# Second front's Abs and Exp spread over scan steps, q and k weights scaled in other buffers, and the last net with the last pair's outputs computed by halves of the tokens

## The chip, the cores and the metric

The kernel runs on one core of one Trainium2 chip. The metric is the device time of one execution in microseconds (us); lower is better. All data are 32-bit floats. The engines are named as the profile names them: PE (TensorE, matmuls; PEld is its weight loading), DVE (VectorE), ACT (ScalarE), POOL (GpSimd), SP (SyncE, which only issues DMAs here).

## The reference

Eight sequences of 512 tokens with 256 features go through two layers, each with a layer norm ahead of and behind it and a residual. The first is a state-space layer, the second a mixture-of-experts attention with a feed-forward net.

```python
# layer 1, per sequence: D_INNER = 512 channels, 16 states each
dt = softplus(dt_r @ dt_proj_w.T + dt_proj_b)
h  = exp(dt * A) * h + dt * B * xc          # scan over 512 tokens
y  = (h @ C + xc * D) * silu(z) @ out_proj_w.T
x  = x + norm(y)
# layer 2, per sequence: H = 16 heads of 64, E = 8 experts, top 2 by gate
q, k = rope(src @ Wq), rope(src @ Wk);  gv, go = gate(src)
o    = softmax(q @ k.T / 8) @ (sum over e of gv[e] * (src @ Wv[e]))
src  = ln1(src + sum over heads, e of go[e] * o @ Wo[e])
src  = ln2(src + relu(src @ W1 + b1) @ W2 + b2)     # W1: 256 x 1024
out  = x + norm(src)
```

## The kernel before

**Order.** PE, DVE, ACT and POOL execute in the order in which the program issues to them. That order is made while the program is built: `_Order` (line 98) keeps a clock `now` of planned PE time, and every piece of work is a generator or a callback with a due time. `pe(us)` books PE time, each DVE call books its own cost (`_Vector`, line 165), `yield us` asks to go on so much later, `Free` marks pieces that may go on without waiting for free DVE time. What is due is issued at that point, so a different due time is a different place in the queue of an engine. DMAs are issued by SP (most) and POOL (the accumulating ones); SP's order is left to the framework's scheduler, and its queue is in order as well: an issue that waits for a buffer holds all later ones.

**Buffers.** A pool hands out its buffers per tag in turn: `wpool` two of each tag (`wqk`, `w_m`, `wv`, `wo`, `gb`), `work` two of each (`p`, `ve`, `og`), `big` seven, `half` five, `one` a single one per tag (`dt`, `dtx`, `xc`, `pt`, `o`, `qk`). `psum` has three tiles of two banks, `psum_a` one, which holds the sum over all heads (`sums[b]`).

**State-space layer.** For sequence b, `front(b)` (line 315) makes the inputs and `mamba(b)` (line 492) scans. The scan has 32 steps; a step takes one of 4 blocks of 128 channels and 2 of 16 states, tile 128x1024. A step is one DVE scan (`h<-da,ps_u` or `h<-da,h`) and one DVE product with `ct`, and for later sequences a product ahead of it; ACT makes the decays `da` (two Exp) of the next step; POOL issues two DMAs that add the products into `xc` (line 566). Scan 0 runs nearly alone. During it `front(1)` prepares sequence 1: its Abs (line 457) and Exp (line 459), two groups of two Abs and one Exp, go to ACT between the decays.

**Weights of q and k.** `later_constants` (line 266) loads the q and k weights of each of 8 head pairs into a tile of tag `wqk`, scales the q part on ACT (line 289) and stores it to DRAM `wqk_d` (line 290); from the third on it waits until sequence 0 is in `state`. `Pair.project` (line 803) loads the scaled weights back, into a tile of the same tag.

**Attention.** 8 pairs of heads per sequence. `ahead` (line 1101) issues a pair's values `ps_v`, scores `ps_s`, transposes `ps_pt` and the next pair's projection `ps_qk`, and between them the eight outputs of the pair before, `add_output(k)` (line 967): for each expert two matmuls of 512 tokens into `sums[b]`. Their inputs `og` are DVE products of the pair's result `o` with the gates `gb`, which SP broadcasts from DRAM (`weigh`, line 954).

**Net.** `feed_forward(b)` (line 992) runs among the pairs of sequence b + 1: residual sum, transposes to tokens, norm, transposes to features, `ps_f` with W1 (line 1040) and with W2 (line 1062) in two halves of F, norm, norm, output. For the last sequence nothing is left beside it: after the last pair come its eight outputs and then the net, one after the other.

Of the kernel before, what the change touches and what calls it, by code (L numbers as in the profile page):

```python
# [26 lines left out]
F32 = mybir.dt.float32  # L27
AF = mybir.ActivationFunctionType
ALU = mybir.AluOpType
# [3 lines left out]
P = 128  # L33
B, S, D = 8, 512, 256
ND = D // P
NT = S // P
# [3 lines left out]
H, HP, E, F = 16, 64, 8, 1024  # L40
NF = F // P
# [15 lines left out]
NET, FIRST = -9, 0.2  # L57
# [40 lines left out]
class _Order:  # L98
# [11 lines left out]
    def pe(self, us):  # L110
        self.now += us
        self.here = self.now
# [4 lines left out]
    def after(self, us, do):  # L117

        heapq.heappush(self.queue, (self.here + us, self.n, do))
        self.n += 1  # L120
# [95 lines left out]
def _layers(  # L216
# [3 lines left out]
    nc = tc.nc  # L220
    with ExitStack() as ctx:
        pool = lambda name, bufs, **kw: ctx.enter_context(tc.tile_pool(name=name, bufs=bufs, **kw))
        const = pool("const1", 1)
        wpool = pool("weights", 2)
        seq = pool("seq", 2)
        big = pool("big", 7)
        half = pool("half", 5)
        work = pool("work", 2)
        one = pool("one", 1)
# [7 lines left out]
        x1_d = [tc.dram_tile([P, NT, D], F32, name=f"x1_d_{b}") for b in range(B)]  # L237
# [13 lines left out]
        b1_t = const.tile([P, NF], F32, name="b1_t")  # L251
        rows_t = const.tile([P, 4, D], F32, name="rows_t")
# [13 lines left out]
        def later_constants():  # L266

            nc.sync.dma_start(out=w_sel, in_=wsel)
            nc.sync.dma_start(out=angle[:, :, 0, :], in_=rope)
            half_turn = half.tile([P, P], F32, tag="half", name="half_turn")  # L270
            nc.sync.dma_start(out=half_turn, in_=turn)
            nc.sync.dma_start(out=b1_t, in_=b1)
            nc.sync.dma_start(
                out=rows_t.rearrange("p r d -> p (r d)"),
                in_=rows[:, : 4 * D].to_broadcast([P, 4 * D]),
            )
            yield 8.0


            vector.tensor_reduce(sign, half_turn, AX.X, ALU.add)  # L280
            vector.tensor_scalar(angle[:, 1, 0, :], angle[:, 1, 0, :], sign, None, ALU.mult)

            for i in range(H // 2):
                w = wpool.tile([P, 2, ND, P], F32, tag="wqk", name=f"wqk_s_{i}")
                nc.sync.dma_start(out=w, in_=wqk[i])
                yield 6.0
                while i > 1 and 0 not in state:
                    yield Free(2.0)
                nc.scalar.mul(w[:, 0], w[:, 0], HP**-0.5)
                nc.sync.dma_start(out=wqk_d[i], in_=w)  # L290

        def banks(name):
            return psum.tile([P, 2, S], F32, tag="mm", name=name)
# [18 lines left out]
        state = {}  # L312
        pe, after, then = order_of.pe, order_of.after, order_of.then

        def front(b):
# [4 lines left out]
            free = Free if b == 1 else float  # L320
# [16 lines left out]
            ps = to_features(xn, f"m_{b}")  # L337
# [40 lines left out]
            for m in range(0, NC, 2):  # L378
                ps = project(m)
# [4 lines left out]
            if b == 0:  # L384
                ps = project(NC)
# [42 lines left out]
            if b == 0:  # L428
                ps = project(NC + 2)
# [4 lines left out]
            if b == 0:  # L434
# [8 lines left out]
            nc.sync.dma_start(  # L443
                out=row, in_=bc_d[b][2 * NS : 2 * NS + 1, :].to_broadcast([P, S])
            )
            yield free(1.0)
            if b > 1:
                yield from gate()
            yield free(2.0)
# [4 lines left out]
            for m in range(0, NC, 2):  # L454
                u = tile_for(f"u_{b}_{m}", "og")
                for i in range(2):
                    nc.scalar.activation(u[:, i, :], row, AF.Abs, **step_size(m + i))
                yield free(1.4)
                nc.scalar.activation(u, u, AF.Exp, scale=-1.0)
                us.append(u)  # L460
                yield free(1.1)
            while b == 1 and at["step"] < steps - 1:
                yield Free(0.5)
            for u in us:
                m = 2 * len(lns)
                spare = b == 0 and m
# [10 lines left out]
            for ln, u in zip(lns, us):  # L477
                m = 2 * lns.index(ln)
                for i in range(2):
                    w = half.tile([P, S], F32, tag="half", name=f"w_{b}_{m + i}")  # L480
# [308 lines left out]
        class Pair:  # L789
# [3 lines left out]
            def __init__(self, b, pair):  # L793
                self.b, self.pair, self.id = b, pair, f"{b}_{pair}"
                self.xt = inputs_of[b]
                self.p, self.og = {}, {}

                self.done = set()

            def need(self, *what):  # L800
# [129 lines left out]
            def attend(self):  # L930


                self.need(*((of, t) for of in ("pt", "v") for t in range(NT)))
                po = banks(f"ps_o_{self.id}")
                for t in range(NT):
                    for j in range(2):
                        nc.tensor.matmul(  # L937
                            po[j * HP : j * HP + HP, 0, :], lhsT=self.v[:, j, t, :],
                            rhs=self.pt[:, j, t, :], start=(t == 0), stop=(t == NT - 1),
                        )  # L940
                pe(4.4)
                self.o = one.tile([P, 1, S], F32, tag="o", name=f"o_{self.id}")
                nc.scalar.copy(self.o, po[:, 0:1, :])  # L943
                for q in range(2):
                    after(0.8 + 0.1 * q, lambda q=q: self.weigh_soon(q))

            def weigh_soon(self, q):
# [5 lines left out]

            def weigh(self, q):

                gb = wpool.tile([P, 2, S], F32, tag="gb", name=f"gb_{self.id}_{q}")
                for j in range(2):
                    r = (2 * self.pair + j) * E + 2 * q
                    nc.sync.dma_start(
                        out=gb[j * HP : j * HP + HP].rearrange("p e s -> p (e s)"),  # L960
                        in_=go_d[self.b][r : r + 2, :].rearrange("e s -> (e s)")
                        .unsqueeze(0).to_broadcast([HP, 2 * S]),
                    )
                og = self.og[q] = work.tile([P, 2, S], F32, tag="og", name=f"og_{self.id}_{q}")
                vector.tensor_tensor(og, self.o.to_broadcast([P, 2, S]), gb, ALU.mult)

            def add_output(self, k):

                if self.pair == 0 and k == 0:
                    sums[self.b] = psum_a.tile([P, ND, S], F32, tag="sum", name=f"ps_a_{self.b}")  # L970
                pa, q, i = sums[self.b], k // 2, k % 2
                order_of.run(lambda: q in self.og)
                if i == 0:
                    w = self.wo = wpool.tile(
                        [P, 2, D], F32, tag="wo", name=f"wo_{self.id}_{q}"
                    )
                    for j in range(2):
                        nc.sync.dma_start(
                            out=w[j * HP : j * HP + HP],
                            in_=wo[2 * self.pair + j][:, q, :].rearrange("(i p) d -> p i d", i=2),  # L980
                        )
                for c in range(ND):
                    nc.tensor.matmul(  # L983
                        pa[:, c, :], lhsT=self.wo[:, i, bass.ts(c, P)], rhs=self.og[q][:, i, :],
                        start=(self.pair == 0 and k == 0),
                        stop=(self.pair == H // 2 - 1 and k == E - 1),
                    )
                pe(1.71)
                if i == 1 and q + 2 < E // 2:
                    after(0.05, lambda: self.weigh(q + 2))  # L990

        def feed_forward(b, pa):

# [90 lines left out]
            nc.sync.dma_start(out=out[b].rearrange("(t p) d -> p t d", p=P), in_=z)  # L1084
            finished.add(b)

        sums, prepared, inputs_of = {}, {}, {}  # L1090
        scanning, scanned, through, gated, summed, finished = (set() for _ in range(6))
# [22 lines left out]
                    part()  # L1114
                order_of.run()

        last = None
        with tc.manual_schedule(engines=MANUAL):
            first = front(0)
            order_of.start(first, 0, next(first))  # L1120
            order_of.start(mamba(0), 0)
            order_of.start(front(1), FIRST, 9.0)
            first_constants()
            order_of.run(lambda: 0 in scanning)
            order_of.start(later_constants(), NET)
            order_of.run(lambda: 0 in inputs_of)
            pairs = {}
            follow(-1, H // 2 - 1)
            for b in range(B):
                for pair in range(H // 2):  # L1130
                    now = pairs.pop((b, pair))
                    ahead(now, lambda: follow(b, pair))
                    if pair == 0 and b:
                        order_of.start(feed_forward(b - 1, sums[b - 1]), NET)
                    now.attend()
                    order_of.run()
                    last = now
            for k in range(E):
                last.add_output(k)
                order_of.run()  # L1140
            order_of.start(feed_forward(B - 1, sums[B - 1]), NET)
            order_of.run(lambda: not (order_of.queue or order_of.rest))


# [81 lines left out]
```

## Time and profile before

| | us |
|---|---|
| median of 3 runs | 3695.3 |
| lowest, highest | 3694.61, 3702.96 |
| the profiled execution, its own time | 3698.07 |
| its span, first to last instruction | 3696.3 |
| busy PE, DVE, POOL, ACT | 3413.1, 3047.2, 1681.2, 1645.2 |

The profile shows one execution. A wait is named by the instruction that waits and what it waited for; the chain that ended last follows the end of the span back from each instruction to what released it. A matmul of 32-bit data is two instructions of the profile, so `add_output` shows as four rows of 128x512. The page cuts the span in 40 slices of 92.4 us: PE is busy below 90% in the first five (state-space layer of sequence 0, first pairs) and in the last, which holds the last outputs and the last net.

### The profile page before, as it was taken

Reading aid. Unit: us, or ns where it says so; the run is one execution under the profiler, and the core shown is the slowest. Engines: PE = TensorE matmul, PEld = TensorE weight load, DVE = VectorE, ACT = ScalarE, POOL = GpSimd, SP = SyncE. Lnnn points to the kernel's source line nnn. Section 1 sums busy time; section 2 is a strip of 40 time slices with the busy share of each in tenths; the row PEclk is TensorE's granted clock in tenths of the full one; section 3 lists DMA queues with packets and bytes.
Section 4 is the critical chain, followed back from the end, with each engine's and each line's share of the span. In section 5 each row is a group of like instructions: output and inputs, shape, how many; then the busy total and the mean of one; then the engine's idle time right before and its main releaser. Section 6 shows DMA issues by size and latency. Waiting matters only on the chain.

```text
span 3696.3 us, 34548 instructions
## 1 busy us (share of the span) xinstructions
PE 3413.1 (92%) x10956; PEld 1626.4 (44%) x10956; DVE 3047.2 (82%) x3190; ACT 1645.2 (45%) x2798; POOL 1681.2 (45%) x1593
## 2 busy tenths in 40 slices
PE   5768889999999999999999999999999999999996
PEld 3633334444344444444444544434444444445443
DVE  7878998799989898999989998899988998754443
ACT  5524443545543455344544446443653444332331
POOL 1415663354645545454454545355444556232230
PEclk7879999999999999999999999999999999999998
DMA  4937774576866768477755868568765777344431
GB/s 144 196 93 183 174 176 119 149 186 166 195 150 162 179 168 196 121 182 177 199 142 142 201 149 209 138 152 194 183 168 132 179 191 175 99 120 112 111 92 57
DMA packets 285604, 578.48 MB, mean 157 GB/s; under 512 B 37608, under 2 KB 124904, under 8 KB 285424
## 3 DMA queue, kind: packets, MB, share of 16 engines
q1 hardware_dynamic: 204656, 427.33, 40.0%
q0 software_dynamic: 80768, 148.95, 24.1%
q8 instruction: 89, 1.46, 0.2%
q14 instruction: 91, 0.75, 0.1%
HBM read 405.72 MB, written 21.51 MB: 116 GB/s over the span
## 4 chain that ended last, share of the span: by engine, by line
PE 47%; DVE 26%; issue 8%; DMA 7%; ACT 5%; POOL 5%; SPq 0%; DVEq 0%; POOLq 0%; ACTq 0%
PE ps_v L907 14%; PE ps_a L983 12%; DVE h L175 11%; PE ps_qk L810 5%; DMA xc<-h 5%; PE ps_s L848 4%; PE ps_o L937 3%; PE ps_pt L883 3%; DVE ve L175 2%; DVE og L175 2%; DVE low L175 2%; PE ps_f L1040 1%; DVE xs L175 1%; DVE hit L175 1%; POOL ve L923 1%
## 5 line engine op out<-in xcount | busy, mean ns | idle before, releaser
L983 PE MATMUL ps_a<-og,wo 128*128 128x512 f32 x2048 | 967.1, 605 | 32.8 <-DVE og L175 32.5
L907 PE MATMUL ps_v<-wv,xt 128*128 128x512 f32 x2048 | 946.8, 606 | 21.4 <-DVE y L175 13.2
L923 POOL TENSOR_TENSOR ve<-ve 128x512 f32<-128x512 f32 x256 | 425.3, 1661 | 1144.9 <-DVE ve L175 994.7
L863 ACT ACTIVATE p<-ps_s,low 128x512 f32<-128x512 f32 x512 | 347.3, 683 | 723.6 <-DVE low L175 723.1
L566 POOL DMA_DIRECT2D xc<-h x504 | 465.1, 1103 | 384.7 <-DMA xc<-h 174.6
L907 PEld LDWEIGHTS ps_v<-wv,xt 128*128 128x128 f32 x2048 | 385.6, 193 | 544.8 <-issue 484.2
L983 PEld LDWEIGHTS ps_a<-og,wo 128*128 128x128 f32 x2048 | 373.1, 192 | 506.4 <-issue 429.0
L175 DVE TENSOR_TENSOR_SCAN h<-da,h 128x1024 f32<-128x1024 f32 x228 | 541.0, 2373 | 10.2 <-ACT da L503 0.2
L872 ACT ACTIVATE p<-p,total 128x512 f32<-128x512 f32 x512 | 341.5, 714 | 260.8 <-DVE total L175 260.4
L175 DVE TENSOR_TENSOR og<-o,gb 128x1024 f32<-128x1024 f32 x256 | 319.7, 1269 | 130.3 <-ACT o L943 72.4
L175 DVE TENSOR_TENSOR ve<-ps_v,gv 128x1024 f32<-128x1024 f32 x256 | 311.4, 1216 | 126.5 <-PE ps_v L907 99.3
L889 ACT COPY pt<-ps_pt 128x1024 f32<-128x1024 f32 x256 | 256.9, 1005 | 356.5 <-PE ps_pt L883 355.2
L503 ACT ACTIVATE da<-dt,decay 128x511 f32<-128x511 f32 x512 | 339.7, 713 | 104.6 <-DVE h L175 101.8
L175 DVE TENSOR_TENSOR h<-bt,dtx 128x1024 f32<-128x1024 f32 x228 | 321.2, 1409 | 33.7 <-DMA xc<-h 28.6
L175 DVE TENSOR_TENSOR h<-h,ct 128x1024 f32<-128x1024 f32 x256 | 339.1, 1324 | 3.8
L175 DVE TENSOR_REDUCE low<-ps_s 128x2 f32<-128x1024 f32 x256 | 310.4, 1213 | 26.6 <-PE ps_s L848 25.6
L924 POOL TENSOR_TENSOR ve<-ve 128x256 f32<-128x256 f32 x256 | 319.2, 1247 | 20.1
L832 POOL DMA_DIRECT2D qk<-sin x256 | 204.7, 1212 | 264.5 <-DVE qk L175 127.2
L848 PE MATMUL ps_s<-qk 64*128 64x512 f32 x1024 | 294.2, 650 | 23.7 <-ACT p L863 12.8
L883 PEld LDWEIGHTS ps_pt<-ident,p 128*128 128x128 f32 x2048 | 239.5, 141 | 132.0 <-issue 94.8
L937 PE MATMUL ps_o<-pt,v 128*64 128x512 f32 x1024 | 248.3, 611 | 29.0 <-POOL v L925 16.4
L883 PE MATMUL ps_pt<-ident,p 128*128 128x128 f32 x2048 | 266.7, 273 | 7.6 <-ACT p L872 3.3
(134 smaller groups left out, 3340.3 us busy)
## 6 DMA issues: line engine op xcount, KB each, us to landing
gb<-go_d SPq DMA_DIRECT2D x512, 256.0 KB, 4.9
xc<-h POOLq DMA_DIRECT2D x504, 256.0 KB, 5.7
wv<-in_wv_dram SPq DMA_DIRECT2D x128, 512.0 KB, 5.7
wo<-in_wo_dram SPq DMA_DIRECT2D x512, 128.0 KB, 4.0
ct<-bc_d SPq DMA_DIRECT2D x64, 512.0 KB, 5.9
bt<-bc_d SPq DMA_DIRECT2D x57, 512.0 KB, 5.2
wqk<-wqk_d SPq DMA_DIRECT2D x64, 256.0 KB, 2.6
qk<-sin POOLq DMA_DIRECT2D x256, 64.0 KB, 4.7
```

The source lines that it names most:

```text
L175: return getattr(self.engine, name)(*args, **kw)
L503: nc.scalar.activation(das[k % 2][:, j, 1:S], dt[:, m, 1:S], AF.Exp, scale=decay[:, m, g + j : g + j + 1],)
L566: nc.gpsimd.dma_start(out=xc[:, k % NC, :], in_=hs[k][:, j, :], accum_op=ALU.add)
L848: nc.tensor.matmul(ps[:, j, :], lhsT=self.qk[feats, 0, bass.ts(t, P)], rhs=self.qk[feats, 1, :], start=True, stop=True,)
L863: nc.scalar.activation(p[:, j, :], ps[:, j, :], AF.Exp, bias=low[:, j : j + 1], accum_out=total[:, j : j + 1],)
L872: nc.scalar.mul(p[:, j, :], p[:, j, :], total[:, j : j + 1])
L883: nc.tensor.transpose(pp[:, j, bass.ts(i, P)], self.p[t][:, j, bass.ts(i, P)], ident)
L907: nc.tensor.matmul(ps[:, i, :], lhsT=self.xt[:, c, bass.ts(t + i, P)], rhs=self.wv[:, c, :], start=(c == 0), stop=(c == ND - 1),)
L923: nc.gpsimd.tensor_tensor(ve[:, :, 0:4], ve[:, :, 0:4], ve[:, :, 4:8], ALU.add)
L924: nc.gpsimd.tensor_tensor(ve[:, :, 0:2], ve[:, :, 0:2], ve[:, :, 2:4], ALU.add)
L937: nc.tensor.matmul(po[j * HP : j * HP + HP, 0, :], lhsT=self.v[:, j, t, :], rhs=self.pt[:, j, t, :], start=(t == 0), stop=(t == NT - 1),)
L983: nc.tensor.matmul(pa[:, c, :], lhsT=self.wo[:, i, bass.ts(c, P)], rhs=self.og[q][:, i, :], start=(self.pair == 0 and k == 0), stop=(self. ...
```

## The change

Three edits. (1) `front(1)` waits longer in planned time ahead of its Abs and Exp and between them. (2) The tiles for scaling q and k weights take tag `w_m` in place of `wqk`, and from the third on the wait is for the gates of sequence 0 and stands ahead of the load. (3) For the last sequence, outputs are added by halves of the 512 tokens (`add_half`: matmuls of 256 tokens), the residual enters the sum as a matmul with the identity, and a function `last_net` replaces the last outputs and `feed_forward(7)`: it issues its loads at the start of the last sequence's second pair, into the buffers of `dt`, `dtx` and `xc`, and then runs outputs, norms, W1 and W2 for one half of the tokens beside the other.

```diff
@@ later_constants @@
             for i in range(H // 2):
-                w = wpool.tile([P, 2, ND, P], F32, tag="wqk", name=f"wqk_s_{i}")
+                while i > 1 and 0 not in gated:
+                    yield Free(2.0)
+                w = wpool.tile([P, 2, ND, P], F32, tag="w_m", name=f"wqk_s_{i}")
                 nc.sync.dma_start(out=w, in_=wqk[i])
                 yield 6.0
-                while i > 1 and 0 not in state:
-                    yield Free(2.0)
                 nc.scalar.mul(w[:, 0], w[:, 0], HP**-0.5)
                 nc.sync.dma_start(out=wqk_d[i], in_=w)
@@ front @@
-            yield free(1.0)
+            yield free(12.0 if b == 1 else 1.0)
...
                     nc.scalar.activation(u[:, i, :], row, AF.Abs, **step_size(m + i))
-                yield free(1.4)
+                yield free(3.5 if b == 1 else 1.4)
                 nc.scalar.activation(u, u, AF.Exp, scale=-1.0)
                 us.append(u)
-                yield free(1.1)
+                yield free(3.5 if b == 1 else 1.1)
@@ Pair @@
+                self.final = b == B - 1 and pair == H // 2 - 1
...
-                for q in range(2):
+                for q in range(E // 2 if self.final else 2):
                     after(0.8 + 0.1 * q, lambda q=q: self.weigh_soon(q))
...
-                gb = wpool.tile([P, 2, S], F32, tag="gb", name=f"gb_{self.id}_{q}")
+                spare = self.final and q > 1
+                of, tag = (work, "ve") if spare else (wpool, "gb")
+                gb = of.tile([P, 2, S], F32, tag=tag, name=f"gb_{self.id}_{q}")
...
-                og = self.og[q] = work.tile([P, 2, S], F32, tag="og", name=f"og_{self.id}_{q}")
+                og = self.og[q] = work.tile(
+                    [P, 2, S], F32, tag="p" if spare else "og", name=f"og_{self.id}_{q}"
+                )
...
+                if self.b == B - 1:
+                    for g in range(2):
+                        self.add_half(k, g, self.wo[:, i])
+                else:
...
+            def add_half(self, k, g, w):
+                pa = sums[self.b].rearrange("p g (c s) -> p g c s", c=ND)[:, g]
+                if self.pair == 0 and k == 0:
+                    nc.tensor.matmul(
+                        pa, lhsT=ident, rhs=self.xt[:, :, bass.ts(g, S // 2)],
+                        start=True, stop=False,
+                    )
+                    pe(0.86)
+                for c in range(ND):
+                    nc.tensor.matmul(
+                        pa[:, c, :], lhsT=w[:, bass.ts(c, P)],
+                        rhs=self.og[k // 2][:, k % 2, bass.ts(g, S // 2)],
+                        start=False, stop=(self.final and k == E - 1 and c == ND - 1),
+                    )
@@ new @@
+        def last_net():
+            b = B - 1
+            w_1 = one.tile([P, ND, F], F32, tag="dt", name="w1_last")
+            w_2 = one.tile([P, NF, D], F32, tag="dtx", name="w2_last")
+            w_o = one.tile([P, E // 2, 2, D], F32, tag="xc", name="wo_last")
+            x1 = big.tile([P, NT, D], F32, tag="big", name="x1_last")
+            b2 = half.tile([P, 1, D], F32, tag="half", name="b2_last")
+            for j in range(2):
+                nc.sync.dma_start(
+                    out=w_o[j * HP : j * HP + HP],
+                    in_=wo[H - 2 + j].rearrange("(i p) q d -> p q i d", i=2),
+                )
+            nc.sync.dma_start(out=w_1, in_=w1)
+            nc.sync.dma_start(out=w_2, in_=w2)
+            nc.sync.dma_start(out=x1, in_=x1_d[b])
+            nc.sync.dma_start(out=b2[:, 0, :], in_=rows[:, 4 * D :].to_broadcast([P, D]))
+            yield
+            pa = sums[b].rearrange("p g (c s) -> p g c s", c=ND)
+            half_of = lambda name: [
+                big.tile([P, ND, S // 2], F32, tag="big", name=f"{name}_last_{g}") for g in (0, 1)
+            ]
+            wide = [P, NT // 2, D]
+            rows_of = lambda i: rows_t[:, i : i + 1, :].to_broadcast(wide)
+            acc, y, yt = half_of("acc"), half_of("y"), half_of("yt")
+            hid = one.tile([P, NF, S], F32, tag="pt", name="hid_last")
+            def outputs(g, ks):
+                for k in ks:
+                    order_of.run(lambda: k // 2 in last.og)
+                    last.add_half(k, g, w_o[:, k // 2, k % 2])
+                    pe(0.86)
+                    order_of.run()
+            def to_tokens(g):
+                ps = banks("ps_acc_last")[:, 0, :].rearrange("p (t d) -> p t d", d=D)
+                for t in range(NT // 2):
+                    for c in range(ND):
+                        nc.tensor.transpose(
+                            ps[:, t, bass.ts(c, P)], acc[g][:, c, bass.ts(t, P)], ident
+                        )
+                nc.scalar.copy(y[g], ps)
+            def normed(g, *then):
+                for _ in norm(y[g], [y[g][:, t, :] for t in range(NT // 2)]):
+                    pass
+                for a, op in then:
+                    vector.tensor_tensor(y[g], y[g], a, op)
+            def features(g):
+                ps = banks("ps_tr_f_last")
+                for c in range(ND):
+                    for t in range(NT // 2):
+                        nc.tensor.transpose(
+                            ps[:, c, bass.ts(t, P)], y[g][:, t, bass.ts(c, P)], ident
+                        )
+                nc.scalar.copy(yt[g], ps[:, :, : S // 2])
+                vector.tensor_tensor(y[g], y[g], b2.to_broadcast(wide), ALU.add)
+            def hidden(g, f):
+                ps = banks("ps_f1_last").rearrange("p a (i s) -> p (a i) s", s=S // 2)
+                for i in range(4):
+                    for c in range(ND):
+                        nc.tensor.matmul(
+                            ps[:, i, :], lhsT=w_1[:, c, bass.ts(f + i, P)], rhs=yt[g][:, c, :],
+                            start=(c == 0), stop=(c == ND - 1),
+                        )
+                for i in range(4):
+                    nc.scalar.activation(
+                        hid[:, f + i, bass.ts(g, S // 2)], ps[:, i, :], AF.Relu,
+                        bias=b1_t[:, f + i : f + i + 1],
+                    )
+            def second(g):
+                ps = banks("ps_f2_last")[:, 0, :].rearrange("p (t d) -> p t d", d=D)
+                for t in range(NT // 2):
+                    for f in range(NF):
+                        nc.tensor.matmul(
+                            ps[:, t, :], lhsT=hid[:, f, bass.ts(g * NT // 2 + t, P)],
+                            rhs=w_2[:, f, :], start=(f == 0), stop=(f == NF - 1),
+                        )
+                vector.tensor_tensor(y[g], y[g], ps, ALU.add)
+                normed(g, (rows_of(2), ALU.mult), (rows_of(3), ALU.add))
+                tiles = slice(g * NT // 2, (g + 1) * NT // 2)
+                normed(g, (x1[:, tiles, :], ALU.add))
+                nc.sync.dma_start(
+                    out=out[b].rearrange("(t p) d -> p t d", p=P)[:, tiles, :], in_=y[g]
+                )
+            first = ((rows_of(0), ALU.mult), (rows_of(1), ALU.add))
+            outputs(0, range(E))
+            outputs(1, range(2))
+            nc.scalar.copy(acc[0], pa[:, 0])
+            outputs(1, range(2, 4))
+            to_tokens(0)
+            outputs(1, range(4, E))
+            normed(0, *first)
+            nc.scalar.copy(acc[1], pa[:, 1])
+            features(0)
+            to_tokens(1)
+            hidden(0, 0)
+            normed(1, *first)
+            hidden(0, 4)
+            features(1)
+            for f in range(0, NF, 4):
+                hidden(1, f)
+            for g in range(2):
+                second(g)
@@ main loop @@
-        last = None
+        last, net = None, last_net()
...
                 for pair in range(H // 2):
+                    if (b, pair) == (B - 1, 1):
+                        next(net)
...
-            for k in range(E):
-                last.add_output(k)
-                order_of.run()
-            order_of.start(feed_forward(B - 1, sums[B - 1]), NET)
-            order_of.run(lambda: not (order_of.queue or order_of.rest))
+            order_of.run(lambda: not order_of.rest)
+            next(net, None)
```

## The prediction

> **What bounds the kernel now.** I read the page's busy line and its 40 slices first, then PE's waits, then the timelines of the three places that the edits touch.
>
> ```profile
> PE 3413.1 (92%) x10956; PEld 1626.4 (44%) x10956; DVE 3047.2 (82%) x3190; ACT 1645.2 (45%) x2798; POOL 1681.2 (45%) x1593
> ...
> PE   5768889999999999999999999999999999999996
> ```
>
> PE bounds all but the ends: slices 6 to 39 are at 90% or more. Three places can give time without less matmul work: scan 0 (the 5 and 7, bound by DVE), the few waits of the early pairs, and the last slice.
>
> Scan 0 is bound by DVE: a step takes 3.45 us there, and PE waits for it. In DVE's and ACT's timelines the second front's Abs and Exp show as a stall of one step:
>
> ```profile
> 123.10 2.29 DVE L175 TENSOR_TENSOR_SCAN h<-da,ps_u 128x1024 f32<-128x1024 f32 x1 [3.13 <-ACT da L503]
> ```
> ```profile
> 117.83 1.52 ACT L457 ACTIVATE u<-row,chan,w_dt 128x512 f32<-128x512 f32 x2 [3.88 <-DMA row<-bc_d]
> 119.38 1.06 ACT L459 ACTIVATE u<-u 128x1024 f32<-128x1024 f32 x1
> 120.34 1.50 ACT L457 ACTIVATE u<-row,chan,w_dt 128x512 f32<-128x512 f32 x2
> ...
> 132.33 1.33 ACT L503 ACTIVATE da<-dt,decay 128x511 f32<-128x511 f32 x2 [1.54 <-DVE h L175]
> ```
>
> Start and length come first, the bracket is the idle time and its end. Two Abs, an Exp and two Abs stand in one row ahead of the decays `da`, 4.1 us without a gap, and the scan waits 3.13. The last row is an undisturbed step: ACT has 1.54 free.
>
> In the first pairs of sequence 0 one wait of PE is for the weights of q and k:
>
> ```profile
> 272.26 5.25 PE L810 MATMUL ps_qk<-xt,wqk 128*128 128x512 f32 x8 [5.51 <-DMA wqk<-wqk_d]
> ```
> ```profile
> 266.99 0.41 ACT L289 ACTIVATE wqk_s<-wqk_s 128x256 f32<-128x256 f32 x1
> ```
>
> The load of pair 1's weights waits until the scaling of another pair's is stored, because both use two buffers of one tag: scaled at 266.99 + 0.41, store and load behind each other, PE free to go on at 266.75 and started at 272.26.
>
> The end is a chain with PE and DVE in turn (from the chain of waits, start, length, work):
>
> ```profile
> 3642.92 1.95 PE ps_tr_f L300 x8
> ...
> 3645.96 9.73 PE ps_f L1040 x16
> 3655.69 7.24 PE ps_f L1062 x32
> 3662.93 6.87 PE ps_f L1040 x16
> 3669.79 7.25 PE ps_f L1062 x32
> ...
> 3677.07 1.23 DVE y L175
> ```
>
> From 3631.8 (last output) to 3645.96 PE has 3 us of work; the same 16 matmuls that take 6.87 later take 9.73 after that pause.
>
> **Edit 1, Abs and Exp.** Nothing is removed but the place. One Abs pair (1.52) or one Exp (1.06) fits in a step's 1.54. So the 3.13 goes. What is late next is the pool of four `h` buffers, freed by POOL's accumulating DMAs. DVE's timeline has two such stalls soon after, 2.71 at 175.26 and 3.93 at 189.65 ("DMA xc<-h"), and the 16 DMA engines are busy 0.82, 0.99 and 1.04 of the time at 120–130, 130–140 and 160–170. If the adds are the limit, DVE comes to the same wait earlier and the gain is given back. Bounds: −3.1 (all kept) to +2 (about the 1.8 that the step after the next would wait even without a stall). I take −1.0, nearer to the transfers' row, since the share is about 1.
>
> **Edit 2, weights of q and k.** Removed: the shared tag. In the built order of the changed program pair 1's load is issued before the scan of sequence 0 ends, at about 95 us. Then `ps_qk` can go at 266.8 (−5.5), and at full clock its 8 rows take 3.6 and not 5.25 (−1.6): together −7.1. DVE behind it waits 6.74 for `ps_qk` (277.62), which goes. One ACT scaling (0.42) leaves the chain too, −7.5 in all. What may be late next is the gates' chain `go`→`gb`→`og` (292.24 to 298.99), which moves with it. Added: six scalings (ACT 0.41 each), six loads and six stores of 256 KB fall together in pair 1; on SP's queue each store waits for its scaling and later issues wait behind it, about 2.4. 3 MB cost 10.8 us of the 16 engines' time (427.33 MB in 40.0% of 3696.3: 0.289 MB per us), in a stretch with shares up to 0.89. Bounds −7.6 to −2; I take −6.0.
>
> **Edit 3, ahead of the tail.** (a) The loads: two of 1 MB (W1, W2), two of 512 KB (Wo), one of 512 KB. In the built order SP issues W1 at about 3112.6 and W2 at about 3118.7, beside the last accumulations of the last scan. Wo waits for `ps_out` of sequence 7 (3147.2) and falls where the engines idle. The rows there (window, length, PE, PEld, DVE, ACT, POOL, granted clock, DMA share, GB/s):
>
> ```profile
> 3116.00:3120.00 4.00, 4.00 (x15) 2.04 (x15) 4.00 (x4) 3.67 (x7) 2.02 (x3) 1.00 1.08 261
> 3124.00:3128.00 4.00, 4.00 (x10) 1.71 (x9) 2.40 (x3) 1.45 (x4) 3.10 (x5) 1.00 0.30 65
> 3140.00:3144.00 4.00, 4.00 (x14) 3.22 (x13) 0.00 (x0) 0.00 (x0) 0.00 (x0) 0.67 0.00 0
> ```
> ```profile
> 3139.50 7.84 PE L676 MATMUL ps_out<-w_out,xc 128*128 128x256 f32 x28 [2.64 <-DVE xc L175]
> ```
>
> The share is 1.08 at first, so 2 MB (7.2 us of all engines) delay the adds by something between nothing (the 0.30 of 3124–3128 takes them up) and 7.2; the last add lands at 3138.1, and PE waits for it already (2.64). I take +2.5; the bounds are 0 and +7.2, and 1.5 more if the clock stays at 0.67 longer. No other work covers it: PE's queue is in order.
>
> (b) Sequence 7 in halves, beside PE at 100%: the identity adds four rows of 0.43 (2 × 2), +1.72. Rows of 256 columns cost 0.2159 (32 in 6.91 us from 3332.46), 512 cost 0.4294: 2 × 0.2159 − 0.4294 = 2.4 ns for each of some 224 rows, +0.5. The net of sequence 6 has its rows in another order, with ACT's copy of its tokens behind a `p` scaling that waits for DVE: +1.1 (0 to 3). Sum +3.4 (2.2 to 5). Removed at no gain, as DMAs hide: eight Wo loads, four of W.
>
> **Edit 3, the tail.** Before: first outputs with the last `og` at 3617.23, DVE done at 3692.0, span 3696.3. After, step by step:
> - Half 0: 32 rows × 0.216 = 6.9, to 3624.1. Half 1 and four transposes of half 0: to 3631.5. No wait for Wo (0.25 and 2.84 before).
> - Norm of half 0 on DVE: half of before's rows, 2.50 (statistics, 1.1 of POOL, two scalings 0.7) + 1.26 (two products) and its ACT copy 0.6; mostly beside PE's half 1, done 3633.4. Transposes, copy of 0.6: W1 starts at 3634.8, 11.2 earlier than before.
> - Four groups of W1 at 16 × 0.216 = 3.45: 13.8; the copy for half 1 stands behind eight Relu on ACT, a gap of 1.65 (estimate from before's 1.27 for two Relu of 512). W2 of half 0: 6.9, to 3657.3.
> - Then DVE: sum 0.64, norm 2.50 + 0.71, products 1.26, norm 2.50 + 0.71, sum 0.64 = 8.96 for a half. It has to do this twice, one after the other, 17.9 (before 14.9 at once, from 3677.07): 3657.3 + 17.9 = 3675.2. PE's last W2 (3664.2) is hidden behind it.
> - The same 4.3 after it. So 3692.0 − 3675.2 = −16.8.
>
> That holds at full clock. After half 1 PE idles about 2 us and then has little work until 3634.8. The rows: 1.94 idle at 3615.3 left the clock at 1.00, 2.64 idle at 3136.9 brought 0.67. I take one cold stretch, 1.7: −15.1, with bounds −17.2 (a shorter last store too) and −11.5 (cold through W1, the 2.9 that before lost, and a Relu gap twice as long).
>
> The Trainium skill, "TensorE: Matmul & The Clock Gate", section "Part 1: The HAM clock gate", lets the clock fall to half after at least one idle window of about 3.4 us. By that rule this tail (2 us idle) would have no cold stretch and the term would be −16.8; the row with 2.64 idle and a clock of 0.67 speaks against it, and I go by the row.
>
> **Sum.** −1.0 − 6.0 + 2.5 + 3.4 − 15.1 = −16.2. The profiled execution's own time is 3698.1, so 3681.9; it lies 2.8 above the median of the runs, 3695.3, which makes 3679.1. I say 3679.0.
>
> **Rivals.**
> - *Transfers and clock take most of the tail's gain* (0.22). W1 and W2 delay the adds by 6 in place of 2.5, PE's pause there is then over 8 us and the clock stays low into the next pair (+1.5), the tail runs cold (−11.5), edit 1 gives nothing: 0 − 6 + 7.5 + 3.4 − 11.5 = −6.6: 3688.7, within 0.3%. For: the share 1.08. Against: the 0.30 right after it and all those rows of 0.00 at 3140.
> - *All covers hold* (0.12): −3.1 − 7.5 + 0 + 2.2 − 17.2 = −25.6: 3669.7. For: ACT's 1.54 free in each step; against: the shares near 1 beside scan 0.
> - *Slower* (0.05): the wait for the weights of q and k is not removed but moved to the later pairs, as their six scalings are now all behind the gates of sequence 0. A pair that catches its weights unscaled pays the scaling 0.4, the store 2.0 and the load 2.7, 5.1: before's way from 266.99 to 272.14. Three such pairs leave nothing but 0.9 of the 16.2; at four the kernel is slower, by over 0.3% only at six, which make +14.4: 3709.7. Against: with both `w_m` buffers free, six times 5.1 end some 31 us after the gates, by 346; the pairs follow each other by 48 us or so, the first needs its weights at 324.9.
> - *The edit doesn't do what it says* would be a last net whose DVE chain is the longer one: it is (17.9 against 14.9), and stands in the sum; if PE's W2 of half 1 came late by over 9, nothing of the order would pay. No row points there.
>
> **Numbers.** My forecast has 0.61, centre 3679.0, its own range 3671 to 3686. 0.3% is 11.1 us, about what a measurement of this kernel can tell from no change. Faster by more: below 3684.2, most of the forecast's 0.61 (0.56) and the 0.12: 0.68. Within: the 0.22 and the 0.05 left of the forecast: 0.27. Slower: 0.05. The range, 3668 to 3691, takes in the forecast, the rival of the transfers and most of the better case.
>
> **What would show it.** Right: no "DVE h <- ACT da" of 3.1 near 123, and larger or earlier "DMA xc<-h" waits; no "PE ps_qk <- DMA wqk"; PE's wait for `xc` at the last scan's end above 2.64 and below 6; from the first rows with the last `og` to the span's end 64 in place of 79. Wrong: PE waiting for wqk in pairs 2 to 7, more than 5 us between the last row of half 1 and W1, DVE's last chain above 18, or a wait above 8 for `xc` at 3137.

## The result and the profile after

The changed kernel takes 3681.59 us (median of 6 runs, 3672.64 to 3686.95), the kernel before 3696.88 (6 runs). The ratio is 0.9956, 95% interval 0.9941 to 0.9970: 16.3 us less, by the interval 11 to 22. The prediction, 3679.0 and 16.2 less, holds in time and sign; of its terms two were wrong by 2.5 and more, in opposite ways. The profiled execution of the changed kernel was its slowest, 3686.95 (span 3685.2).

The page of the changed kernel, busy time and PE's 40 slices:

```profile
PE 3414.7 (93%) x11248; PEld 1683.7 (46%) x11248; DVE 3049.3 (83%) x3198; ACT 1647.6 (45%) x2810; POOL 1679.0 (46%) x1596
...
PE   5768889999999999999999999989999999999997
```

PE does the same work in a shorter span. The last slice goes from 6 to 7, the first ones stay.

Scan 0 in DVE's timeline of the changed kernel (start, length, instruction, idle time before and its end):

```profile
93.23 2.29 DVE L175 TENSOR_TENSOR_SCAN h<-da,ps_u 128x1024 f32<-128x1024 f32 x1 [2.95 <-DMA xc<-h]
...
123.81 2.28 DVE L175 TENSOR_TENSOR_SCAN h<-da,ps_u 128x1024 f32<-128x1024 f32 x1
...
128.85 2.29 DVE L175 TENSOR_TENSOR_SCAN h<-da,ps_u 128x1024 f32<-128x1024 f32 x1 [1.51 <-DMA xc<-h]
```

The stall of 3.13 for `da` is gone. 1.51 of it comes back two steps later as a wait for the adds. The row at 93.23 is the surprise: it stands ahead of anything that edit 1 moves, and the same step waited less in the kernel before:

```profile
90.62 2.29 DVE L175 TENSOR_TENSOR_SCAN h<-da,ps_u 128x1024 f32<-128x1024 f32 x1 [1.16 <-DMA xc<-h]
```

Pair 1's projection in PE's timeline:

```profile
269.50 3.70 PE L812 MATMUL ps_qk<-xt,wqk 128*128 128x512 f32 x8
```

No wait, and full speed (3.70 in place of 5.25). Pairs 2 to 7 don't wait for `wqk` either.

The end of scan 7: DMA share is the second column from the right, then PE's row with its wait:

```profile
3116.00:3120.00 4.00, 3.72 (x17) 1.72 (x15) 4.00 (x4) 2.97 (x7) 0.37 (x1) 1.00 0.96 296
3124.00:3128.00 4.00, 4.00 (x11) 1.75 (x10) 2.43 (x3) 1.34 (x3) 2.60 (x4) 1.00 1.01 345
```
```profile
3137.72 7.96 PE L676 MATMUL ps_out<-w_out,xc 128*128 128x256 f32 x28 [2.52 <-DVE xc L175]
```

The hole of 0.30 at 3124 is filled to 1.01, and the wait is the same, 2.52 against 2.64.

The tail in PE's timeline, and three rows of the chain that ended last (start, length, work):

```profile
3613.17 3.65 PE L939 MATMUL ps_o<-pt,v 128*64 128x512 f32 x16
3618.77 10.59 PE L1013 MATMUL ps_a<-og,wo_last 128*128 128x256 f32 x40 [1.95 <-DVE og L175]
3630.03 1.99 PE L1013 MATMUL ps_a<-og,wo_last 128*128 128x256 f32 x8 [0.68 <-ACT acc_last L1208]
...
3638.96 8.86 PE L1179 MATMUL ps_f_last<-yt_last,w_last 128*128 128x256 f32 x32 [0.24 <-ACT yt_last L1172]
...
3649.95 7.17 PE L1179 MATMUL ps_f_last<-yt_last,w_last 128*128 128x256 f32 x32 [1.70 <-ACT yt_last L1172]
3656.96 13.98 PE L1193 MATMUL ps_f_last<-w_last,hid_last 128*128 128x256 f32 x64
```
```profile
3657.13 6.92 PE ps_f_last L1193 x32
...
3664.07 0.70 DVE y_last L175
...
3681.04 0.69 DVE y_last L175
```

From the first W2 rows' end, 3664.05, DVE's chain (with POOL's part of the norms) sets the end: 17.7 for two halves to the end of its last row, as forecast (17.9). Two groups of PE ran with a low clock: 40 output rows in 10.59 in place of 8.9, and 32 rows of W1 in 8.86 in place of 7.17 (the shorter times are those of e10, below).

### The profile page after: what moved, and what is told of

Its sections match the earlier page's. It is cut to its first block, busy times and chain, and to the rows that moved or that the text cites. A ratio compares the mean times of both kernels' runs of the same rounds, so it can differ in the third digit from the quotient of the medians.

```text
span 3685.2 us, 35142 instructions
## 1 busy us (share of the span) xinstructions
PE 3414.7 (93%) x11248; PEld 1683.7 (46%) x11248; DVE 3049.3 (83%) x3198; ACT 1647.6 (45%) x2810; POOL 1679.0 (46%) x1596
## 4 chain that ended last, share of the span: by engine, by line
PE 48%; DVE 27%; issue 8%; DMA 7%; ACT 5%; POOL 4%; SPq 0%; DVEq 0%; POOLq 0%; ACTq 0%
PE ps_v L909 14%; DVE h L175 11%; PE ps_a L993 9%; DMA xc<-h 5%; PE ps_qk L812 5%; PE ps_s L850 4%; PE ps_a L1013 3%; PE ps_o L939 3%; PE ps_pt L885 3%; DVE low L175 2%; DVE og L175 2%; DVE ve L175 2%; PE ps_out L676 1%; DVE xs L175 1%; DVE hit L175 1%
## 5 line engine op out<-in xcount | busy, mean ns | idle before, releaser
L909 PE MATMUL ps_v<-wv,xt 128*128 128x512 f32 x2048 | 943.9, 604 | 19.4 <-DVE y L175 11.5
L993 PE MATMUL ps_a<-og,wo 128*128 128x512 f32 x1792 | 847.7, 606 | 30.6 <-DVE og L175 30.5
L993 PEld LDWEIGHTS ps_a<-og,wo 128*128 128x128 f32 x1792 | 326.8, 192 | 444.7 <-issue 368.8
```

Of the source, the lines that this page charges most:

```text
L909: nc.tensor.matmul(ps[:, i, :], lhsT=self.xt[:, c, bass.ts(t + i, P)], rhs=self.wv[:, c, :], start=(c == 0), stop=(c == ND - 1),)
L993: nc.tensor.matmul(pa[:, c, :], lhsT=self.wo[:, i, bass.ts(c, P)], rhs=self.og[q][:, i, :], start=(self.pair == 0 and k == 0), stop=(self. ...
```

## The experiments

All times are ratios to the kernel before on the same chip; 0.001 is 3.7 us. One execution differs from the next by several us in sequences 1 to 6, which nothing here changes before 3112 us: between pair 3 of sequence 0 (372 us) and pair 4 of sequence 6 (3033 us) one profile (e5) gained 11.5 us on the kernel before and another (the changed kernel) 0.1. Over the twelve profiles this stretch takes 2648.3 to 2662.8 us. By the trace's record of the granted clock, PE's clock stood at half for 81.9 to 111.1 us of it, and a line through the twelve pairs of numbers rises by 0.50 us per us (correlation 0.87): most of the spread goes with the time at the half clock, and up to some 4 us either way do not. So single effects of 2 us are read from the stage where they arise, over several profiles, and the times only bound them.

### Each edit alone

e1 is the kernel before with edit 1, e2 with edit 2, e3 with edit 3; e4 has edits 2 and 3 (their diffs are the parts of the diff above).

> Edit 1 alone on the kernel before. Theory A (transfers limit scan 0, what the spread saves comes back as waits for the adds, and the loads that move with it cost more): +1 to +3.5 us, scan 0 ends later than before, the 3.1 us wait for da gone, a wait for xc in its place. Theory B (the spread itself gains, what is lost in the changed kernel before its 113 us comes from edit 2's early load of q and k weights): -1.5 to -3, and the waits up to 113 us as in the kernel before.

> Edit 2 alone on the kernel before. Theory A: -6 to -7.1 us, scan 0 as before, the 5.5 us wait of PE for wqk gone. Theory B: -2.5 to -4 us, because scan 0 itself gets 2 to 3.6 us longer by the early load beside the adds.

> Edit 3 alone on the kernel before. My sum: +2.5 + 3.4 - 15.1 = -9.2 us; from the changed kernel's trace: +2.6 ahead of the tail and -12.6 in it, -10.0. If the clock in the tail stays at 1.00 in this run, 3 to 4 us better (-13.5). Rival (the loads of 2 MB cost the last scan): the wait for xc at the end of scan 7 is over 5 us.

> The changed kernel with edit 1 undone (edits 2 and 3 kept). Theory A: 1 to 3.5 us below the changed kernel, ratio to before about 0.9950. Theory B: 1.5 to 3 us above the changed kernel, ratio about 0.9963.

| kernel | edits | ratio, interval | pair 0 starts | pair 0 to 1 | pair 1 to 3 |
|---|---|---|---|---|---|
| before | none | 1 | 229.73 | 42.53 | 100.33 |
| e3 | 3 | 0.9970, 0.9959 to 0.9981 | 232.86 | 42.09 | 102.88 |
| e1 | 1 | 0.9995, 0.9986 to 1.0004 | 230.73 | 42.54 | 100.60 |
| e2 | 2 | 0.9989, 0.9981 to 0.9998 | 234.17 | 37.19 | 101.11 |
| e4 | 2, 3 | 0.9956, 0.9944 to 0.9968 | 233.98 | 37.10 | 101.62 |
| changed | 1, 2, 3 | 0.9956, 0.9941 to 0.9970 | 233.37 | 36.13 | 101.57 |

The last three columns are the starts of PE's `ps_qk` rows in us, and their distances. Pair 0's start has 16 rows of `ps_sel` ahead of it that took 5.13 us in the kernel before and 6.74 in the changed one, so the end of scan 0 is better read from DVE's last product there (`xc<-ps_y`). Its start, as the mean of the profiles of a kind (e5 to e10 are described below):

| second front's weights loaded | without edit 1 | with edit 1 |
|---|---|---|
| early | 201.3 (before, e3) | 199.6 (e1, e5, e9) |
| late, by edit 2 | 204.4 (e2, e4) | 201.9 (changed, e6, e7, e8, e10) |

Profiles of one kind lie up to 2.3 apart. By these traces theory A falls: edit 1 costs nothing. Alone its time is 1.8 less, by the interval between 5.2 less and 1.5 more, which reaches into A's range. In e1 the wait of 3.13 is gone, and what stands in its place is 1.35 for PE's `ps_u`, not a wait for `xc`. Edit 2 gains 5 between pairs 0 and 1 as forecast, and scan 0 ends 2.3 to 3.1 later with it, as theory B said; which transfer does it was open. The times decide neither: e2 is 4.1 less (0.7 to 7.0), and e4 has the changed kernel's ratio, between the 0.9950 of A and the 0.9963 of B. e3 is 11.1 less (7.0 to 15.1), about as expected, and its wait for `xc` at the end of scan 7 is 2.62, so its rival falls.

### Which transfer lengthens scan 0

SP's timeline, the kernel before:

```profile
32.61 0.54 SPq L353 DMA_DIRECT2D w_in<-in_m_in_dram  x1
...
43.42 0.55 SPq L353 DMA_DIRECT2D w_in<-in_m_in_dram  x1
```

and the changed kernel:

```profile
33.40 0.33 SPq L287 DMA_DIRECT2D wqk_s<-in_wqk_dram  x1
...
43.40 0.74 SPq L287 DMA_DIRECT2D wqk_s<-in_wqk_dram  x1
...
83.81 0.56 SPq L353 DMA_DIRECT2D w_in<-in_m_in_dram  x1
...
94.38 0.55 SPq L353 DMA_DIRECT2D w_in<-in_m_in_dram  x1
```

The input weights `w_in` of a front (line 352) have tag `w_m`, too. The first two scalings now take those buffers until their stores at 80 and 88, and the second front's weights are loaded only then, beside the adds. e5 gives only the later six scalings the new tag:

```diff
-w = wpool.tile([P, 2, ND, P], F32, tag="w_m", name=f"wqk_s_{i}")
+w = wpool.tile([P, 2, ND, P], F32, tag="w_m" if i > 1 else "wqk", name=f"wqk_s_{i}")
```

> The changed kernel, but the first two scalings keep tag wqk and only the six later ones take w_m. Theory: edit 2 lost part of its 7.1 us because with w_m for the first two SP issues the second front's w_in loads (512 KB) only among the adds of scan 0 (84 and 94 us in place of under 60); with the old tag for these two the loads go back to their old place, the scan's wait for xc before its seventh-last ps_u group at 93 us goes from 2.7-2.95 back to 1.2, the one after it (0.55) goes, and PE still does not wait for wqk: 2.3 us below the changed kernel, ratio to before about 0.9950. Rival: the longer wait is due to pair 1's wqk load (94.9 us), which stays early here: then the waits stay at 2.7 to 3.0 and the time at the changed kernel's.

e5, SP's and DVE's timelines:

```profile
32.25 0.54 SPq L353 DMA_DIRECT2D w_in<-in_m_in_dram  x1
...
43.07 0.55 SPq L353 DMA_DIRECT2D w_in<-in_m_in_dram  x1
...
92.31 0.32 SPq L808 DMA_DIRECT2D wqk<-wqk_d  x1
```
```profile
90.19 2.29 DVE L175 TENSOR_TENSOR_SCAN h<-da,ps_u 128x1024 f32<-128x1024 f32 x1 [1.13 <-DMA xc<-h]
```

The loads are back at 32 and 43 and the wait is 1.13, though pair 1's weights are still loaded early (92.3): the rival falls. Scan 0's last product starts at 199.2, and at 198.7 in e9, which has the same edit, against 200.9 to 202.5 in the five profiles with edit 1 and late loads. Pair 0 starts at 228.86, pair 1 37.16 later. Over the profiles the waits for `xc` between 88 and 102 us sum to 1.2 or less where `w_in` is early (before, e1, e3, e5; none in e9) and to 2.9 to 3.5 where it is late (seven profiles). The ratio is 0.9959 (0.9946 to 0.9972), forecast 0.9950: the time alone does not show it.

### The clock in the tail

e6 adds work that nobody uses where PE idled:

```diff
+def fill():
+    ps = banks("ps_fill")
+    for i in range(2):
+        nc.tensor.matmul(ps[:, i, :], lhsT=ident, rhs=w_1[:, i, :S], start=True, stop=True)
...
+fill()
 outputs(0, range(E))
...
+fill()
 features(0)
```

> The changed kernel with two matmuls with the identity (four rows of 0.43 us, results not used) in each of two places of the tail where PE idles: between the last ps_o and the first outputs (1.95 us), and ahead of the transposes of half 0 (1.73 us). Theory (an idle stretch under 2 us costs the clock): the first 40 output rows take 8.7 in place of 10.59 and 32 rows of W1 7.2 in place of 8.86: 1.9 to 3.6 us below the changed kernel, ratio about 0.9948. Rival (the 64 columns of ps_o and other light work lower the clock, not the idle time): the rows stay at 10.6 and 8.9 and the time is the same or up to 0.5 us longer.

PE's timeline of e6:

```profile
3602.62 1.98 PE L1153 MATMUL ps_fill<-w_last,ident 128*128 128x512 f32 x4
3604.63 8.90 PE L1013 MATMUL ps_a<-og,wo_last 128*128 128x256 f32 x40
...
3623.13 7.17 PE L1186 MATMUL ps_f_last<-yt_last,w_last 128*128 128x256 f32 x32 [0.24 <-ACT yt_last L1179]
```

Both groups run at full speed. Ratio 0.9954 (0.9941 to 0.9966). From the end of the last `ps_o` (its start and length added) to the span's end it is 64.9 us, in the changed kernel's profile 68.4. But a second profile of the changed kernel, e10, was at full speed with no filling:

```profile
3613.89 8.90 PE L1013 MATMUL ps_a<-og,wo_last 128*128 128x256 f32 x40 [1.94 <-DVE og L175]
...
3632.39 7.17 PE L1179 MATMUL ps_f_last<-yt_last,w_last 128*128 128x256 f32 x32 [0.24 <-ACT yt_last L1172]
```

and it, too, has 65.0. Without filling, the outputs after the 1.94 idle were slow in 8 of 10 profiles (before and e10 were not), and W1 of half 0 was slow in 3 of 7 with the new tail. So the idle time allows the low clock and does not force it; with filling it was absent in 2 of 2 (e6, e9).

What goes with the slow groups can be read from the trace's record of the granted clock. In every profile it stands at 1.00 or 0.50 and changes only at times that are whole multiples of 3.41 us apart; where these times fall differs from profile to profile. The stretch with the pause and the next one, in the changed kernel and in e10 (window, length, PE, PEld, DVE, ACT, POOL, granted clock, DMA share, GB/s):

```profile
3615.55:3618.97 3.42, 1.48 (x7) 0.35 (x4) 1.48 (x2) 0.59 (x1) 0.00 (x0) 1.00 0.00 0
3618.97:3622.38 3.41, 3.41 (x9) 2.66 (x9) 3.15 (x3) 0.00 (x0) 0.00 (x0) 0.50 0.00 0
```
```profile
3610.43:3613.85 3.42, 1.52 (x8) 0.29 (x4) 1.24 (x2) 0.58 (x1) 0.00 (x0) 1.00 0.00 0
3613.85:3617.26 3.41, 3.37 (x16) 2.98 (x17) 3.39 (x3) 0.00 (x0) 0.00 (x0) 1.00 0.00 0
```

In the eight profiles with slow outputs the whole pause of 1.94 or 1.95 lies in one such stretch, and the next stretch has the half clock. In before and e10 the end of a stretch cuts the pause, and the stretch holds 1.80 and 1.90 of it. Ahead of W1 of half 0 a stretch holds 1.80 to 1.90 us of idle time in the three slow profiles and at most 1.56 in the other four. With filling no stretch from the last `ps_o` to W1 holds more than 0.68. `ps_o` stands ahead in all twelve, so its light work alone does not lower the clock. So the place of the pause accounts for all these cases, though for the outputs by as little as 0.04 us, and no run moved that place on purpose. How much idle time it takes is not shown: 1.90 ahead of the outputs was too little, and 1.80 ahead of W1, with transposes in the rest of the stretch, was enough.

### The order of the tail

e7 puts W2 of half 0 ahead of W1 of half 1:

```diff
 features(1)
+second(0)
 for f in range(0, NF, 4):
     hidden(1, f)
-for g in range(2):
-    second(g)
+second(1)
```

> The changed kernel with W2 of half 0 ahead of W1 of half 1 in the tail. Theory (the tail's end is two DVE chains of 8.9 in a row after the first W2, PE done 11 us before the end): half 0's chain runs beside PE's W1 and W2 of half 1, features of half 1 are copied beside W2 of half 0 (the 1.7 us gap goes), and the end is PE's last W2 plus one chain: 3.5 us below the changed kernel (ratio about 0.9947). Rival (PE would end the tail anyway, or the chain of half 0 is late): within 1 us of the changed kernel.

PE's timeline of e7, and DVE's row after it:

```profile
3645.88 7.07 PE L1193 MATMUL ps_f_last<-w_last,hid_last 128*128 128x256 f32 x32
3652.79 7.07 PE L1179 MATMUL ps_f_last<-yt_last,w_last 128*128 128x256 f32 x32
3659.70 7.07 PE L1193 MATMUL ps_f_last<-w_last,hid_last 128*128 128x256 f32 x32
```
```profile
3666.80 0.69 DVE L175 TENSOR_TENSOR y_last<-y_last,ps_f_last 128x512 f32<-128x512 f32 x1 [4.97 <-PE ps_f_last L1193]
```

PE has no gap, and DVE waits for PE (4.97) where it was behind it. With the same two slow groups as in the changed kernel's profile, 64.5 from `ps_o`'s end in place of 68.4: 3.9 less, forecast 3.5. Ratio 0.9943 (0.9929 to 0.9957).

### How much cover the loads had

e8 loads W1 and W2 of the last net twice.

```diff
-nc.sync.dma_start(out=w_1, in_=w1)
-nc.sync.dma_start(out=w_2, in_=w2)
+for _ in range(2):
+    nc.sync.dma_start(out=w_1, in_=w1)
+    nc.sync.dma_start(out=w_2, in_=w2)
```

> The changed kernel with W1 and W2 of the last net each loaded twice into the same tiles, 2 MB more beside the last adds of scan 7. Theory (the loads cost nothing as they filled the hole of 0.30 DMA share at 3124 to 3128, which is now full): the adds land later, PE's wait for xc at the end of scan 7 grows from 2.5 to 5 to 9 us, the time by 3 to 7 us. Rival (the loads never delay the adds, whatever their size): the wait stays at 2.5 and the time at the changed kernel's.

PE's row at the end of scan 7 and the windows before it, in e8:

```profile
3130.10 8.27 PE L676 MATMUL ps_out<-w_out,xc 128*128 128x256 f32 x28 [6.28 <-DVE xc L175]
```
```profile
3120.00:3124.00 4.00, 3.82 (x20) 2.36 (x18) 0.22 (x1) 2.02 (x2) 3.37 (x4) 1.00 1.04 333
3124.00:3128.00 4.00, 0.00 (x0) 0.00 (x0) 0.00 (x0) 0.00 (x1) 0.00 (x0) 0.91 1.07 287
```

The engines are full until the adds have landed, and PE waits 6.28: 3.8 more for 2 MB more. Ratio 0.9965 (0.9953 to 0.9976). So the rival falls: the time up to the last add had room for about 2 MB, and the next 2 MB cost half of the 7.2 that I had estimated for as much.

### Together

e9 has the edits of e5, e6 and e7, e10 is the changed kernel once more on the same chip.

> The changed kernel with the three edits of e5, e6 and e7 together (first two scalings with tag wqk, the two fillings of the tail, W2 of half 0 ahead of W1 of half 1). If their gains add: 2.1 (the scan's waits for xc) + 1.7 to 3.4 (clock) + 3.8 (W2 early) = 7.6 to 9.3 us below the changed kernel, ratio to before about 0.9934; from the end of the last ps_o to DVE's last row 57.7 us in place of 63.2 to 64.9. If they do not add (the shorter tail is bound by DVE's first norms): 59 or more.

> The changed kernel itself once more, on the same chip as e9, for a second profile and more times. My sum with what the traces showed: 0 to -2 (edit 1), -3.4 (edit 2), 0 (loads), +3.2 (identity and halves), -12.6 to -15.4 (tail, by whether W1 runs cold): -13 to -18 us, ratio about 0.9957. In its scan 0 the wait for xc before 95 us is over 2 us; from the end of the last ps_o to DVE's last row 63.2 or 64.9 us.

e9: 0.9940 (0.9926 to 0.9954), median 3675.1; e10: 0.9954 (0.9942 to 0.9966), median 3681.5. In e9 DVE's last row ends 57.7 after `ps_o`, as the sum of the three said, and pair 0 starts at 228.47. e9 has the lowest median of its chip; the intervals overlap, so that it beats the changed kernel rests on the traces. By the two ratios it is 5.2 us below e10, less than the 7.6 to 9.3 forecast; the forecast ratio of 0.9934 lies in its interval. e10's wait for `xc` before 95 us is 2.12, and its tail has 61.5 to DVE's last row, less than either forecast value, since neither group was slow.

## Why the prediction was right, step by step

- **Edit 1, −1.0, measured about −2.1.** Scan 0 ends 1.7 earlier with it where `w_in` is loaded early (201.3 to 199.6) and 2.5 earlier where it is loaded late (204.4 to 201.9). With profiles of one kind up to 2.3 apart this shows the sign and hardly the size, and the times do not resolve it. The reason held in part: in the changed kernel 1.51 of the 3.13 came back two steps later as a wait for the adds; I had taken two thirds for lost.
- **Edit 2, −6.0, measured about −3.4.** The mis-sized term. The wait went (pair 0 to 1: 42.4 to 36.9 on the mean, −5.5), and of the 1.6 that I gave to the full clock 0.6 were left by pair 3 (pair 1 to 3: 101.3 to 100.7 on the mean). What failed is the step "Removed: the shared tag": I asked who waits for the old tag's buffers, not who else lives in the new one. `w_in` does, and the wait reappeared in scan 0 as +2.7 (the mean of 3.1 without edit 1 and 2.3 with it). e5 takes it away.
- **Edit 3, loads, +2.5, measured 0.** My lower bound: PE's wait for `xc` at the end of scan 7 is 2.2 to 2.8 in the eight profiles with these loads (e8 aside) and 2.3 to 2.6 in the three without. The row with a share of 0.30 was there to read; I weighted the 1.08 ahead of it more. e8 shows that it was not free space without end.
- **Edit 3, halves, +3.4, measured +3.2.** Between the `ps_qk` rows of pairs 1 and 3 of sequence 7, across the identity rows and the net of sequence 6, it is 118.4 us in the changed kernel, e3 and e4 and 115.7 in the kernel before; 0.4 more come by the last pair's `ps_o`.
- **Tail, −15.1, measured −14.8 on the mean.** From the end of the last `ps_o` to the span's end: 81.0, 82.0 and 82.1 in before, e1 and e2; 68.4, 68.4, 66.7, 66.7, 66.5 and 65.0 in the changed kernel, e3, e4, e5, e8 and e10. The number of slow groups (two, two, one, one, one, none) makes these steps of 1.7. I had one cold stretch in the changed kernel and compared with a profile whose outputs happened to be fast. At full clock (e10) DVE's last row ends 61.5 after `ps_o`, where I had 59.9, and 3.4 follow it, where I had 4.3. I left out PE's wait of 0.68 for ACT's copy of half 0's sum, and half 0's W2 is 0.9 late behind W1's groups.

By these the sum is −2.1 − 3.4 + 0 + 3.2 − 14.8 = −17.1, and the ratio gives −16.3 (11 to 22 less). That the forecast is so close is partly luck: edit 2 was 2.6 too good, and the loads 2.5 and edit 1 1.1 too bad. The signs that I named came as forecast, but for the wait for `xc` at 3137, which I wanted above 2.64, and the 64 us from the first rows with the last `og` to the span's end: 66.4 in the changed kernel's profile, with two slow groups, and 63.0 in e10, with none. Of the rivals, the one with the loads had its mechanism shown in e8, with twice the loads; the slower one found no wait in any later pair.

The Trainium skill, "TensorE: Matmul & The Clock Gate", section "Part 1: The HAM clock gate", says that an idle window of some 3.4 us lowers the clock and that the window runs free of the program. The traces agree with a free window of that length: the granted clock changes only at times that are whole multiples of 3.41 us apart, and these times differ from profile to profile. But the window need not be idle as a whole: 1.94 us of idle time in it were enough in 8 of 10 profiles, and 1.90 and 1.80 were not in the other two with the same instructions ahead; the measurement decides as to the length.

What stays open: the part of the spread in sequences 1 to 6, up to some 4 us either way, that the time at the half clock does not account for, and how much idle time in a stretch brings the half clock.

## What to carry to other kernels

Moving a buffer to another tag moves the wait to the other users of that tag: list them with the times at which they load. A transfer that is hoisted costs what the hole does not hold, so the shares of every window up to its deadline count, and not the first one. When two halves are worked beside each other, ask which engine has the last two chains in a row, and put the first half's producer early enough that they don't stand behind each other (e7: 3.9 us for a change of order).

## What the runs showed of the hardware

A pause of PE of 1.94 us after the last `ps_o` was followed by 1.7 us of loss over 40 rows (10.59 in place of 8.90) in 8 of 10 profiles (over 16 longer rows in two of them, 8.83 in place of 7.13), with a granted clock of 0.62 in the window 3618 to 3622 of the changed kernel, and a pause of 1.73 us with some work of PE behind it did the same to W1 in 3 of 7. The granted clock was 0.50 or 1.00 and changed only at times that are whole multiples of 3.41 us apart, and the same pause cost 1.7 us where it lay whole in one such stretch and nothing where an end cut it. In 2650 us that no edit touches, the time at the half clock differed by up to 29 us between profiles (81.9 to 111.1), and each us of it went with 0.50 us more time. Two MB of loads beside accumulating transfers at a DMA share of 1.0 cost nothing measurable, two more 3.8 us.
